# When the rows of h are requested, and which queue loads a tile's records, in a sparse graph attention layer

## The chip, the cores and the metric

One NeuronCore of a Trainium2 chip runs the whole kernel as one launch. The metric is the time of the device in microseconds (us), lower is better. The five engines are named as in the profile: PE (TensorE, matrix products and transposes), PEld (its weight loads), DVE (VectorE), ACT (ScalarE), POOL (GpSimd) and SP (SyncE, which here only issues DMAs). Each engine executes its own instructions in the order in which the built program lists them.

## The reference

```python
def layer_norm(x, scale, bias):
    mu = jnp.mean(x, axis=-1, keepdims=True)
    var = jnp.mean(jnp.square(x - mu), axis=-1, keepdims=True)
    return (x - mu) * jax.lax.rsqrt(var + EPS) * scale + bias

hs = layer_norm(x, ln1_scale, ln1_bias)          # 4096 x 512
ht = layer_norm(h_target, ln1_scale, ln1_bias)   # 4096 x 512
q = (ht @ Wq + bq).reshape(T, 8, 64) / sqrt(64)
k = (hs @ Wk + bk).reshape(S, 8, 64)
v = (hs @ Wv + bv).reshape(S, 8, 64)
logits = jnp.einsum('thd,shd->hts', q, k)
logits = jnp.where(adj[None] != 0, logits, NEG)
ctx = jnp.einsum('hts,shd->thd', softmax(logits), v).reshape(T, 512)
ht = layer_norm(ht + ctx @ Wo + bo, ln2_scale, ln2_bias)
ff = gelu(ht @ W1) @ W2                          # 512 -> 2048 -> 512
out = layernorm(x + ht + ff)
```

All numbers are float32. The adjacency is 4096 x 4096 int32 with about 17 ones in a row: each target row attends to few sources. The node mask, all ones here, is left out above.

## The kernel before

**Two stages.** In the first, up to about 300 us, the keys and values of all source rows are computed and written to a DRAM table `kvd` (one row of 1024 numbers for each source), while VectorE and ScalarE turn the rows of the adjacency into lists of neighbours. The target rows are sorted by their number of neighbours, in two halves (16 tiles of 128 rows each, A and B), and a record of each row (its degree, its index TGT, the scale and shift of its first norm, up to 24 neighbours) is scattered to DRAM in the sorted order. The lists of the second half are finished during the second stage, up to about 680 us.

**The second stage** goes through 32 tiles of 128 target rows. A tile has between 11 and 39 slots, a slot being one neighbour for each of its 128 rows. The slots are taken three at a time: a slot group (the list `SG`, 211 of them). The steps that the text speaks of, with their lines in the profile:

- *Record load* (L978, tile `rec`, seven buffers): the 128 records of a tile are loaded from DRAM. `prefetch` issues it two tiles ahead, on GpSimd's queue for the first two tiles and on SyncE's for the others. The buffer comes free when the output rows of the tile seven before have been scattered, since the scatter takes its indices from the record.
- *Request of h* (L964, a helper that issues every indirect gather; tile `tq`, three buffers): the 128 rows of `h_target` that the record names, by an indirect DMA on GpSimd's queue.
- *Norm of h* (L990, ScalarE), four transposes (L994, PE), their copies with scale and bias (L997, ScalarE), the product with Wq (L1003, PE) and the scaled q (L1008, VectorE). The generator `front` issues these steps one by one; each `yield` in it is a turn, and there are two turns for each slot group.
- *Requests of kv* (L964, tile `kv`): one indirect gather of 128 rows (512 KB) for each slot into a ring of 17 places (20 from half B on), issued by `issue(k)` four slot groups ahead of their use (five in half B).
- *Logits and values*: the product of q with the keys (L1197) and its sums (L1201) on VectorE, the exponentials on ScalarE (L1205, L1214 and L1178), the values weighted on VectorE (L1161, L1165) and, for the third slot of a group, on ScalarE (L1181, eight instructions), and the sum over the slots by accumulating transposes on PE (L1169, tile `cps`).
- *End of a tile* (`finish`): the sums' reciprocals (L1073, L1079, L1081, L1084), h added by transposes of `tq` (L1092) and the product with Wo (L1096), which are the last readers of that `tq` buffer, then the second norm and its transposes (L1122).
- *Feed-forward* (`feed`): tiles in pairs, with the products L1304 (w1) and L1313 (w2) on PE and the gelu (L1307) on ScalarE. ScalarE loads a table each time it changes between gelu and the exponentials. The rows of x are requested (L964, tile `xt`), the last norm is taken (L1260 to L1277) and the output rows are scattered by an indirect DMA on GpSimd's queue (L1281, `out_dram`).

**Order.** The attention and the feed-forward are generators; `_weave` takes the one with the smaller sum of estimated costs next, and so writes the order of the program. The framework's scheduler then places each engine's instructions by that order as a priority and by when their inputs and buffers are ready in its own estimate, so that an instruction can stand earlier in its engine's queue than the program asks. The order is fixed when the kernel is built. Where buffers are reused, the waits follow from the framework.

In the kernel before, `issue(k)` for the first slot group of a tile issues, in this order, the record load of the tile two ahead, the request of its own h (which begins its `front`), and its first kv requests:

```python
if j0 == 0:
    prefetch(i + 2)
    if i not in tqs:
        fronts[i] = front(i)
        step(fronts, i)
```

Of the kernel before, what the change touches and what calls it, by code (L numbers as in the profile page):

```python
# [17 lines left out]
P = 128  # L18
# [360 lines left out]
RW = E0 + RE  # L379
# [64 lines left out]
def adj_resnorm_kernel(  # L444
# [33 lines left out]
    nc = tc.nc  # L478
# [22 lines left out]
    NA, NBT = len(CAPS_A), len(CAPS_B)  # L501
# [11 lines left out]
    recs_d = [dram.tile([n * P, RW], I32, name=f"rec{i}") for i, (_, n) in enumerate(PARTS)]  # L513
# [19 lines left out]
    with tc.tile_pool(name="keep", bufs=1) as keep:  # L533
# [17 lines left out]
        with ExitStack() as late:  # L551
# [409 lines left out]
            recs, tqs, h2Ts, done, ready = {}, {}, {}, set(), []  # L961
# [6 lines left out]
            def prefetch(i):  # L968
                if i >= NT or i in recs:
                    return  # L970
                r0 = TILES[i][0]
                part = 1 if r0 >= PARTS[1][0] * P else 0
                assert part in done
                r0 -= PARTS[part][0] * P
                rec = sp.tile([P, E0 + MAXE], I32, name="rec", bufs=7)

                eng = nc.gpsimd if i < 2 else nc.sync
                eng.dma_start(rec[:, :RW], recs_d[part][r0:r0 + P, :])  # L978
                recs[i] = rec

            def front(i):


                rec = recs[i]
                tq = sp.tile([P, 2 * D], F32, name="tq", bufs=3)
                t = tq[:, :D]
                gather(t, h_target, rec[:, TGT:TGT + 1])
                yield
                m = rec[:, RST:RST + 2].bitcast(F32)
                nc.scalar.activation(t, t, AF.Identity, bias=m[:, 1:2], scale=m[:, 0:1])  # L990
                yield
                pt = ps.tile([P, KC, P], F32, name="t", bufs=2)
                for kc in range(KC):
                    nc.tensor.transpose(pt[:, kc, :], t[:, kc * P:(kc + 1) * P], ident)  # L994
                hT = tq[:, D:].rearrange("p (c t) -> p c t", c=KC)
                for kc in range(KC):
                    nc.scalar.activation(hT[:, kc, :], pt[:, kc, :], AF.Identity,  # L997
                                         bias=b1r[:, kc:kc + 1], scale=s1c[:, kc:kc + 1])
                yield
                yield  # L1000
                pq = ps.tile([P, D], F32, name="t", bufs=2)
                for kc in range(KC):
                    nc.tensor.matmul(pq, hT[:, kc, :], wq[:, kc, :], start=kc == 0,  # L1003
                                     stop=kc == KC - 1)
                yield
                yield
                yield
                nc.vector.scalar_tensor_tensor(tq[:, :D], pq, HD ** -0.5, bqr,  # L1008
                                               op0=ALU.mult, op1=ALU.add)
                tqs[i] = tq  # L1010


            SG = [(i, j0, min(S, cap - j0)) for i, (_, cap) in enumerate(TILES)
                  for j0 in range(0, cap, S)]
            kvs, rests, fronts = {}, {}, {}
            place = [0]
            for i, _, n in SG:
                if place[-1] + n > RING[i >= NA]:
                    place[-1] = 0
                place.append(place[-1] + n)  # L1020
            first_b = next(k for k, (i, _, _) in enumerate(SG) if i >= NA)
            issued = [0]

            def step(gens, i):

                if i in gens and next(gens[i], StopIteration) is StopIteration:
                    del gens[i]

            def request(k):
# [3 lines left out]
                while issued[0] <= min(k + ahead, len(SG) - 1):  # L1033
# [3 lines left out]
                        assert not mine & set(range(place[m], place[m] + SG[m][2]))  # L1037
                    issued[0] += 1

            def issue(k):  # L1040

                i, j0, n = SG[k]
                if j0 == 0:
                    prefetch(i + 2)
                    if i not in tqs:
                        fronts[i] = front(i)
                        step(fronts, i)
                    if TILES[i][1] > RE:
                        rests[i] = rest_of(i)
                        next(rests[i])  # L1050
                elif j0 + n > 12 and i in rests:
                    for _ in rests.pop(i):
                        pass
                kvs[k] = ring[:, place[k]:place[k] + n, :]
                for j in range(n):
                    gather(kvs[k][:, j, :], kvd[0:N + 1, :], recs[i][:, E0 + j0 + j:E0 + j0 + j + 1])

            def finish(i, p, cps, group, hs, mv):


                rec, tq, cap = recs[i], tqs.pop(i), TILES[i][1]
# [33 lines left out]
                for c in range(KC):  # L1095
                    nc.tensor.matmul(pa, ct[:, c, :], wo[:, c, :], start=False,  # L1096
                                     stop=c == KC - 1, skip_group_check=True)
                yield
                h = sp.tile([P, D], F32, name="h")
                nc.scalar.copy(h, pa)  # L1100
# [33 lines left out]
            def first_fronts():  # L1134

                for i in range(EARLY):
                    prefetch(i)
                for i in range(EARLY):
                    fronts[i] = front(i)
# [216 lines left out]
                for g in gens:  # L1356
                    yield from g

            EARLY = 2
            WAIT = 40.0  # L1360
            AHEAD = 4
            UNIT = 60.0
# [102 lines left out]
```

## Time and profile before

| | |
|---|---|
| median of 4 runs | 1855.67 us (1853.2 to 1859.01) |
| the profiled execution's own time | 1857.45 us |
| its span, first to last instruction | 1855.6 us |
| mean granted TensorE clock | 0.956 |
| busy: PE, DVE, ACT, POOL | 91%, 77%, 65%, 52% of the span |
| kv requests (L964) | 603, 746.9 us busy, 1239 ns each in the mean |
| requests of h (L964, tile tq) | 32, median 962 ns |
| record loads on SyncE (L978) | 30, 14.5 KB each, median 320 ns |
| record loads on GpSimd (L978) | 2, 585 ns each |
| norms of h (L990) | 32, median 813 ns |

How to read it: all durations come from one execution, recorded by the hardware profiler. Busy is the time in which an engine executes, without the time in which it waits. "Idle before" is the time that an engine stood before an instruction, with the instruction or DMA that released it. PE's busy time is that of a pipeline: two products that overlap count once. The granted clock is the share of TensorE's full speed that the chip allowed. A line such as L964 is that of a helper, so its instructions are told apart by their tiles.

### The profile page before, as it was taken

How to read it: one execution, taken by the hardware profiler on the slowest of the kernel's cores; microseconds unless marked ns; L12 is line 12 of the kernel's file. 1: busy time of each engine (PE TensorE's matmuls, PEld its weight loads, DVE VectorE, ACT ScalarE, POOL GpSimd, SP SyncE). 2: the span in 40 equal slices, each digit the busy share in tenths (PEclk: the TensorE clock that was granted, in tenths of full speed). 3: DMA queues.
4: the chain of work that ended last, by engine and by line, in shares of the span. 5: the costliest groups of instructions: out<-in, count | busy, mean ns of one | idle time of the engine just before them, and what ended most of it. 6: DMA issues, size and time to landing. Idle time of an engine off the chain costs nothing. (4 is left out here: it accounts for less than half of the span.)

```text
span 1855.6 us, 22978 instructions
## 1 busy us (share of the span) xinstructions
PE 1692.0 (91%) x7030; PEld 1105.2 (60%) x7030; DVE 1429.3 (77%) x2596; ACT 1211.0 (65%) x3111; POOL 956.5 (52%) x804
## 2 busy tenths in 40 slices
PE   7989874697988989999998989799999999999995
PEld 3434432465655656767666666576666666656663
DVE  6989855999989838777968999788979698778000
ACT  5767634577877637676768877676868677756211
POOL 1000143835546577647568788766667566643101
PEclk9999987789989999999999999899999999999998
DMA  9999959978876648768778788778677776763000
GB/s 351 363 374 378 346 165 345 355 265 328 303 269 204 233 121 304 256 227 276 255 265 304 270 300 301 245 260 263 221 249 243 250 261 217 249 206 114 23 0 25
DMA packets 147757, 463.28 MB, mean 250 GB/s; under 512 B 24468, under 2 KB 29160, under 8 KB 147624
## 3 DMA queue, kind: packets, MB, share of 16 engines
q0 software_dynamic: 95696, 342.19, 54.0%
q1 hardware_dynamic: 44112, 96.44, 14.7%
q10 hardware_dynamic: 7816, 23.08, 3.3%
q8 instruction: 58, 0.95, 0.2%
q14 instruction: 75, 0.61, 0.1%
HBM read 430.76 MB, written 30.89 MB: 249 GB/s over the span
## 5 line engine op out<-in xcount | busy, mean ns | idle before, releaser
L964 POOL DMA_INDIRECT kv<-kvd,rec x603 | 746.9, 1239 | 406.3 <-PE cps L1169 163.1
L1313 PE MATMUL po<-w,gt 128*128 128x512 f32 x1024 | 469.4, 601 | 8.0 <-ACT gt L1307 7.2
L1304 PE MATMUL pf<-h2T,w 128*128 128x256 f32 (+1 forms) x2176 | 470.2, 370 | 0.0
L1197 DVE TENSOR_TENSOR kv<-kv,tq 128x1536 f32<-128x1536 f32 (+2 forms) x211 | 352.1, 1676 | 110.3 <-DMA kv<-kvd,rec 96.1
L1304 PEld LDWEIGHTS pf<-h2T,w 128*128 128x128 f32 x2176 | 392.9, 193 | 66.6 <-issue 21.1
L1181 ACT ACTIVATE kv<-kv,pa 128x64 f32<-128x64 f32 x1520 | 391.4, 336 | 4.5
L1201 DVE TENSOR_REDUCE lg<-kv 128x24 f32<-128x1536 f32 (+2 forms) x211 | 350.3, 1667 | 6.8 <-ACT pa L1178 5.6
L1313 PEld LDWEIGHTS po<-w,gt 128*128 128x128 f32 x1024 | 190.1, 193 | 206.0 <-issue 197.5
L1169 PEld LDWEIGHTS cps<-ident,kv 128*128 128x128 f32 x2008 | 240.7, 146 | 108.3 <-issue 51.5
L1169 PE MATMUL cps<-ident,kv 128*128 128x128 f32 x2008 | 265.2, 281 | 42.2 <-DVE kv L1161 37.0
L1161 DVE TENSOR_TENSOR kv<-kv,p 128x1024 f32<-128x1024 f32 (+1 forms) x211 | 250.7, 1193 | 18.1 <-ACT p L1205 11.5
L687 POOL TENSOR_TENSOR n_rs<-n_ve,mhalf 128x2 f32<-128x2 f32 (+2 forms) x51 | 53.0, 1039 | 354.5 <-DVE n_ve L680 188.7
L728 ACT ACTIVATE kv<-kv 128x1024 uint8<-128x1024 int32 x128 | 134.8, 1054 | 81.3 <-DMA kv<-in_adj_dram 40.6
L929 PE MATMUL pq<-wk,h2T 128*128 128x512 f32 x256 | 125.7, 635 | 12.8 <-ACT tq L931 5.9
L1307 ACT ACTIVATE gt<-pf 128x512 f32<-128x512 f32 x128 | 76.3, 596 | 91.9 <-PE pf L1304 88.5
L735 DVE MAX8 cand<-kv 128x8 uint16<-128x103 uint16 (+1 forms) x640 | 129.8, 251 | 0.5
L1307 ACT ACT_TABLE_LOAD x99 | 127.0, 1283 | 1.6
L1003 PE MATMUL t<-wq,tq 128*128 128x512 f32 x256 | 118.8, 606 | 9.1 <-ACT tq L997 8.5
L1205 ACT ACTIVATE p<-lg 128x24 f32<-128x24 f32 (+2 forms) x179 | 39.0, 218 | 133.8 <-DVE lg L1201 87.9
L929 PE MATMUL pq<-wv,h2T 128*128 128x512 f32 x256 | 115.2, 593 | 1.5 <-ACT tq L931 1.5
L1096 PE MATMUL t<-wo,rb 128*128 128x512 f32 x256 | 115.5, 592 | 0.0
L990 ACT ACTIVATE tq<-tq,rec 128x512 f32<-128x512 f32 x32 | 26.0, 812 | 110.2 <-DMA tq<-in_L_gnn_h_target_dram,rec 109.8
(156 smaller groups left out, 1572.9 us busy)
## 6 DMA issues: line engine op xcount, KB each, us to landing
kv<-in_adj_dram SPq DMA_DIRECT2D x128, 512.0 KB
kvd<-tq ACTq DMA_DIRECT2D x24, 512.0 KB
kv<-kvd,rec POOLq DMA_INDIRECT x603
kv<-in_L_gnn_h_target_dram SPq DMA_DIRECT2D x32, 256.0 KB
kv<-in_x_dram SPq DMA_DIRECT2D x15, 512.0 KB
rest_d<-gid SPq DMA_DIRECT2D x32, 160.0 KB
w<-in_L_gnn_W_dram SPq DMA_DIRECT2D x4, 1024.0 KB
kvd<-kv ACTq DMA_DIRECT2D x8, 512.0 KB
```

What stands on the lines that cost most here:

```text
L728: nc.scalar.activation(sg, a, AF.Sign, accum_out=dpart[:, i, h:h + 1])
L735: nc.vector.max(cand[:, h * SQ + s, :], wd[:, w0:w1])
L929: nc.tensor.matmul(pkv, hT[:, kc, j * P:(j + 1) * P], w[:, kc, :], start=kc == 0, stop=kc == KC - 1)
L964: nc.gpsimd.indirect_dma_start(out=dst, out_offset=None, in_=table[:, :], in_offset=bass.IndirectOffsetOnAxis(ap=idx, axis=0))
L1161: nc.vector.tensor_tensor(v4, v4, p[:, j0:j0 + m, :].unsqueeze(3) .to_broadcast([P, m, H, HD]), ALU.mult)
L1169: nc.tensor.matmul(cps[:, c, :], kv[:, j, D + c * P:D + (c + 1) * P], ident, is_transpose=True, start=j0 + j == 0 and c == 0, stop=j0 + n ...
L1181: nc.scalar.mul(v, v, pa[:, hd:hd + 1])
L1197: nc.vector.tensor_tensor(kv[:, :n, :D], kv[:, :n, :D], tq[:, :D].unsqueeze(1).to_broadcast([P, n, D]), ALU.mult)
L1201: nc.vector.tensor_reduce(lg[:, :n, :], kv[:, :n, :D].rearrange("p j (h d) -> p j h d", h=H), AX.X, ALU.add)
L1304: nc.tensor.matmul(pf[:, k, :], w1[(f0 + k) // KC][:, kc, (f0 + k) % KC * P:((f0 + k) % KC + 1) * P], h2T[:, kc, :w], start=kc == 0, stop= ...
L1307: nc.scalar.activation(gt, pf, AF.Gelu_apprx_tanh)
L1313: nc.tensor.matmul(po[j], gt[:, k, j * P:(j + 1) * P], w2[(f0 + k) // KC][:, (f0 + k) % KC, :], start=False, stop=f0 + k == FC - 1, skip_g ...
```

## The change

The request of h for a tile is issued up to two slot groups sooner: before the kv requests of slot group k, `issue(k)` looks at the groups k+1 and k+2, and where one is the first of a tile, it begins that tile's `front`, provided that the tile three before has had its last product with `tq` issued (`turned`). To make up for it, `front` yields two more turns for each slot group of the lead before the norm, and in half B after its first tile two more in any case. All record loads go to GpSimd's queue. The rest is as before.

```diff
-                eng = nc.gpsimd if i < 2 else nc.sync
-                eng.dma_start(rec[:, :RW], recs_d[part][r0:r0 + P, :])
+                nc.gpsimd.dma_start(rec[:, :RW], recs_d[part][r0:r0 + P, :])
                 recs[i] = rec
 
-            def front(i):
+            def front(i, idle=0):
...
                 gather(t, h_target, rec[:, TGT:TGT + 1])
-                yield
+                for _ in range(1 + idle):
+                    yield
                 m = rec[:, RST:RST + 2].bitcast(F32)
                 nc.scalar.activation(t, t, AF.Identity, bias=m[:, 1:2], scale=m[:, 0:1])
...
+            EARLY = 2
...
+            begun_fronts, turned = set(range(EARLY)), set()
...
+            def begin(i, lead):
+
+                if i not in begun_fronts:
+                    begun_fronts.add(i)
+                    fronts[i] = front(i, 2 * lead + (2 if i > NA else 0))
+                    step(fronts, i)
+
             def issue(k):
 
+                for d in (1, 2):
+                    if k + d < len(SG) and SG[k + d][1] == 0 and SG[k + d][0] - 3 in turned:
+                        begin(SG[k + d][0], d)
                 i, j0, n = SG[k]
                 if j0 == 0:
                     prefetch(i + 2)
-                    if i not in tqs:
-                        fronts[i] = front(i)
-                        step(fronts, i)
+                    begin(i, 0)
...
                     nc.tensor.matmul(pa, ct[:, c, :], wo[:, c, :], start=False,
                                      stop=c == KC - 1, skip_group_check=True)
+                turned.add(i)
                 yield
```

`EARLY = 2` only moves up from further down in the function.

## The prediction

> **What bounds the kernel now.** I read the page first, for the share of each engine and the clock, then the waits, and then, for each place where TensorE stood still, the timeline of all engines around it.
>
> ```profile
> span 1855.6 us, 22978 instructions
> ...
> PE 1692.0 (91%) x7030; PEld 1105.2 (60%) x7030; DVE 1429.3 (77%) x2596; ACT 1211.0 (65%) x3111; POOL 956.5 (52%) x804
> ...
> PE   7989874697988989999998989799999999999995
> ...
> PEclk9999987789989999999999999899999999999998
> ```
>
> TensorE is the bound: from 700 us to 1700 us it is busy in nearly every slice. What can still be won is the few places where it stands, and the half clock that follows such a place (granted clock 0.91 from 1100 to 1200, against 1.00 from 1200 to 1600). The waits say which stream is late:
>
> ```profile
> POOL kv L964 <- PE cps L1169: 163.1, 87, 15.6
> ...
> ACT tq L990 <- DMA tq<-in_L_gnn_h_target_dram,rec: 109.8, 25, 11.7
> ...
> DVE kv L1197 <- DMA kv<-kvd,rec: 96.1, 32, 12.3
> ...
> POOL xt L964 <- DMA out_dram<-xt,rec: 21.8, 13, 4.5
> ...
> PE t L994 <- ACT tq L990: 20.4, 3, 9.6
> ```
>
> The columns are total us, times, longest. The second line is the target of the change: ScalarE stands 109.8 us at the norm of a row block of h (L990) that has not landed. The last line is what TensorE itself loses to it: 20.4 us at three tiles (8, 18 and 20). The largest, tile 20, in the timelines of PE, ACT and POOL:
>
> ```profile
> 1180.11 1.04 PE L1169 MATMUL cps<-ident,kv 128*128 128x128 f32 x8
> 1190.75 1.11 PE L994 MATMUL t<-ident,tq 128*128 128x128 f32 x4 [9.60 <-ACT tq L990]
> ...
> 1189.88 0.81 ACT L990 ACTIVATE tq<-tq,rec 128x512 f32<-128x512 f32 x1 [9.04 <-DMA tq<-in_L_gnn_h_target_dram,rec]
> ...
> 1179.23 3.98 POOL L964 DMA_INDIRECT kv<-kvd,rec  x1 [0.31 <-issue]
> ...
> 1184.77 1.30 POOL L1281 DMA_INDIRECT out_dram<-xt,rec  x1 [0.30 <-issue]
> 1186.38 0.96 POOL L964 DMA_INDIRECT tq<-in_L_gnn_h_target_dram,rec  x1 [0.30 <-issue]
> ```
>
> GpSimd asked for the h rows at 1186.38, with no idle time before it: the request is late because GpSimd's queue is full. In its timeline no gap is over 0.8 us from 1043 to 1196. So an earlier place in that queue helps, and anything put ahead of it hurts.
>
> **The change, part by part.** The order in which the two built kernels issue their instructions, compared queue by queue without a run, tells what moves.
>
> *The h request.* It is asked for sooner in the program, but its tile has three buffers, and it waits for TensorE to be done with the tile three before. Counted in kv requests ahead of it on GpSimd, 29 of the 32 stand within two of where they stood. Tile 18 moves from behind 352 to behind 333 (19 x (1.239 mean + 0.30 gap) = 29 us), tile 19 four sooner, tile 17 six later. On ScalarE the norm keeps its place to a little over one slot group for all but tiles 18, 19 and 30. Tiles 3 and 4 come two requests sooner (3.1 us): VectorE bounds that stretch, so I take nothing, and keep -3.
>
> *The record loads.* Thirty leave SyncE, where they wait 906.2 us for out_dram at L978 with little behind them: once, from 492 to 497 us, an adjacency load stood 4.9 us behind one. That is worth 0 to -4.9; I take 0, since TensorE has no gap over 1.1 us from 445 to 527. The price on GpSimd is in the two that stand there now:
>
> ```profile
> L978 POOL DMA_DIRECT2D rec<-rec x2 | 1.2, 585 | 1.8 <-DMA rec<-R,kv 1.8
> ```
>
> That is 0.585 + 0.30 gap = 0.89 us each, 27 us in all. Neither of the two ran beside VectorE's two-operand products, in which a kv request grows from a median 0.948 to as much as 4.20 us; by that ratio of mean to median (1239/948) a load is 0.76 + 0.30 = 1.06. I take 0.89 and keep 1.06 to 4.5 (4.20 + 0.30) for the range; below nothing it can't be, as each is an instruction more on that queue. They stand in pairs around the x requests, straight ahead of the first h request of a pair of tiles: request, record, x, record, x, h. The wait for an output scatter to land, which the x request bears now (2.24 us at tile 8), passes to the record in front of it and is not new there.
>
> The Trainium skill speaks against this half: "DMA: Bandwidth & Descriptors", section "SWDGE vs HWDGE vs iDMA", gives plain loads to SP or ACT and keeps GpSimd for the irregular ones, and "SBUF — State Buffer", section "SBUF: two separate sides", has a GpSimd DMA's descriptors starve while VectorE holds the shared port. The long kv requests agree; by the rule the change would only lose at every pair.
>
> *The first steps of a tile from 17 on.* On TensorE the transposes (L994) and q products (L1003) of tiles 17 to 31 go one piece of work later, mostly 8 kv transposes (8 x 0.109 = 0.9, by the distance of their starts in the timeline) and 8 passes of L1313 (8 x 0.429 = 3.4) or 16 of L1304 (16 x 0.216 = 3.5): 4.3 us. VectorE's reading of q (L1008) keeps its place among the slot groups.
>
> Now the sum, against the profiled execution's 1857.45 (span 1855.6).
> 1. Tiles 18 and 20. Tile 18's stall (4.96 us) goes with its request 29 us sooner. Tile 20's request comes later by four record loads (3.5) and one x request that now stands before it (1.25): 4.8, so its transposes start at 1195.6. But TensorE by then has done 0.9 + 3.5 + 3.4 + 0.4 + 3.4 = 11.6 us of work (L1169, L1304, L1313, L1092, L1096) that now comes after them. Gain 11.6 - 4.8 = 6.8; tile 18's gain lies inside it, since GpSimd's full queue sets that time. Two gaps become one, and of the 9 us that a clock of 0.91 takes from 100 us I count 3.4 back: -10.2. Bounds: 0 (the stall only moves) and -23 (both gaps and the clock go).
> 2. L1003 stood 2.38, 2.32 and 2.06 us for ScalarE's copy L997 at tiles 26, 27 and 30; one piece later it finds it done: -6.8 (0 if ScalarE slips as far).
> 3. Tile 8 waits already 5.89 us; two record loads more: +1.8.
> 4. Tile 16: the same two loads put the kv rows for 958 us later, and the first slot of tile 15 reached TensorE only 0.6 us ahead: +1.2. At tiles 10, 12 and 14 TensorE reached the transposes 12 to 26 us after the norm, which covers 1.8: nothing.
> 5. Tiles 17 and 19: q is 4.3 us later and VectorE had 1.4 and 2.5 us in hand, so it stands 2.9 and 1.8 where it is 92% busy (147.21 of 160 us): +3.0 of the 4.7, as the reserve ahead of TensorE was 2 to 7 us. From tile 20 on that reserve is 7 us and more: nothing.
> 6. ScalarE gets ten more table loads by the order, at 1.28 us: 12.8 us, all after 760 us. It is 73% busy there, and from tile 20 on 9 us and more ahead of TensorE: nothing. Six fall before 920 us, where the first slot of a tile is only 2 to 3 us ahead: 0 to 7.7, kept for the range.
> Sum: -10.2 - 6.8 + 1.8 + 1.2 + 3.0 = -11.0, so 1846.5 beside the profiled time and 1844.7 beside the median of 1855.67. I say 1846.
>
> **Rivals.**
> *Slower.* The wait for output scatters. From the start of the out_dram request to the release of the next took 5.6 us at tile 8 and 5.5 at 946 us. Where GpSimd now fills that with h and kv requests (tile 20), the records close the gap: 5.5 less one request (1.3) plus 1.8 is 6 us at each of 15 pairs, 90 us of GpSimd. It decides where the kv rows lead VectorE by less than 6 us beyond the 3.4 that a request needs, as from 815 to 960. If a third reaches TensorE, 30 - 17 = +13: 1870. For it: that queue is full for 150 us. Against: 163.1 us in which kv requests wait for TensorE, a cover for most pairs. 0.33.
> *No change.* VectorE at 92% from 1040 to 1200 takes over: gain 1 fails, the rest is -0.8: 1857. 0.17.
> *It does what it says.* If the real clock let the h rows come two slot groups sooner everywhere, L994's 20.4, L1003's 6.8 and half of the half clock go: some -45, 1812. Against it stands the order, in which the requests do not move. 0.07.
> *My sum*, 1833 to 1850: 0.43.
>
> **How the numbers follow.** 0.3% is 5.6 us, about what a measurement of this kernel can tell from no change. Faster is my case and the large one, 0.50; same 0.17; slower 0.33. From my case's gains at their bounds (-23 - 6.8) the low end is 1828; the high end, 1872, takes in the slower rival.
>
> **What would show it.** Right: the PE wait on L990 at tile 18 gone, one gap of about 11 us at tile 20, no gap over 2 us at L1003 after 1400, ScalarE's wait at L990 still near 100 us, 30 record loads under 1.1 us. Wrong: that wait far below 60 us (the requests did come sooner); the record loads waiting 3 us and more each, with VectorE's wait for kv rows well above 96.1 us (the slower rival); VectorE's wait at L1008 well above 38.4 us (part 5 too small).

## The result and the profile after

The changed kernel takes 1855.15 us (median of 52 runs, 1839.59 to 1868.24) against 1858.43 us for the kernel before (median of 78). The ratio is 0.9979, with a 95% interval of 0.997 to 0.9988: 3.9 us less of 1858 by the ratio. The sign is that of the forecast; the forecast gain was 9.7 us beside the median, more than twice as much. The profiled execution of the changed kernel took 1857.43 us, as long as the 1857.45 us of the one before, so the two profiles show where time moved, not how much was won.

The page of the changed kernel, the same rows as were shown of before:

```profile
span 1855.7 us, 22879 instructions
...
PE 1694.8 (91%) x7030; PEld 1105.3 (60%) x7030; DVE 1429.4 (77%) x2596; ACT 1221.6 (66%) x3121; POOL 972.7 (52%) x834
...
PE   7989874697988989999998989989999999999997
...
PEclk9999987698999989999999999999999999999999
```

GpSimd has 30 instructions and 16.2 us more. Of TensorE's waits before, the largest (9.60 us, tile 20) is down to 2.21; one near 990 is longer (5.83 us for 3.18), and others are new: 4.58 us near 902, 3.77 near 1093 and 3.62 near 1309. The waits of the changed kernel:

```profile
POOL kv L964 <- PE cps L1181: 163.9, 79, 16.3
ACT tq L990 <- DMA tq<-in_L_gnn_h_target_dram,rec: 136.2, 27, 12.9
...
DVE kv L1209 <- DMA kv<-kvd,rec: 73.0, 28, 10.9
...
DVE tq L1008 <- PE t L1003: 45.5, 9, 10.0
...
POOL rec L977 <- DMA out_dram<-xt,rec: 28.0, 12, 4.6
...
PE t L1003 <- ACT tq L997: 14.3, 6, 4.6
...
PE t L994 <- ACT tq L990: 9.4, 3, 5.8
```

ScalarE's wait for the h rows grew from 109.8 to 136.2 us: the rows did not come sooner. TensorE's wait at the transposes (L994) fell from 20.4 to 9.4 us, its wait at the q product (L1003) rose from 8.5 to 14.3. The group of the record loads:

```profile
L977 POOL DMA_DIRECT2D rec<-rec x32 | 18.6, 581 | 29.8 <-DMA out_dram<-xt,rec 28.0 <-DMA rec<-R,kv 1.8
```

Each load took 581 ns, as the two of before did (585). The wait for the output scatters stands in front of them now (28.0 us, and 3.5 in front of the x requests, against 21.8 there before). Apart from such waits GpSimd does not stand before a plain load. Its gap of 0.30 us comes before indirect requests only:

```profile
587.67 1.61 POOL L964 DMA_INDIRECT xt<-in_x_dram,rec  x1 [0.31 <-issue]
589.28 0.59 POOL L977 DMA_DIRECT2D rec<-rec  x1
590.16 1.94 POOL L964 DMA_INDIRECT xt<-in_x_dram,rec  x1 [0.30 <-issue]
```

So a load lengthens GpSimd's queue by 0.58 us, and thirty of them by 17 us.

The end of the program differs too. The last lines of PE's timeline, before and after:

```profile
core 0 of [0], span 1855.6 us
...
1828.29 7.03 PE L1313 MATMUL po<-w,gt 128*128 128x512 f32 x16
```

```profile
core 0 of [0], span 1855.7 us
...
1835.82 7.03 PE L1325 MATMUL po<-w,gt 128*128 128x512 f32 x16
```

Before, TensorE ended at 1835.3 and the program 20.3 us later; after, at 1842.8 and 12.9 us later. In this execution TensorE lost 7.5 us and the end gave as much back. The prediction had no term for that end.

### The profile page after: what moved, and what is told of

Same layout as the page of the kernel before. It is cut to its first block, busy times and chain, and to the rows that moved or that the text cites. A ratio compares the mean times of both kernels' runs of the same rounds, so it can differ in the third digit from the quotient of the medians.

```text
span 1855.7 us, 22879 instructions
## 1 busy us (share of the span) xinstructions
PE 1694.8 (91%) x7030; PEld 1105.3 (60%) x7030; DVE 1429.4 (77%) x2596; ACT 1221.6 (66%) x3121; POOL 972.7 (52%) x834
## 5 line engine op out<-in xcount | busy, mean ns | idle before, releaser
L1181 PE MATMUL cps<-ident,kv 128*128 128x128 f32 x2008 | 269.7, 283 | 54.0 <-DVE kv L1173 45.0
L687 POOL TENSOR_TENSOR n_rs<-n_ve,mhalf 128x2 f32<-128x2 f32 (+2 forms) x51 | 48.3, 948 | 345.0 <-DVE n_ve L680 174.3
L1003 PE MATMUL t<-wq,tq 128*128 128x512 f32 x256 | 122.9, 624 | 14.7 <-ACT tq L997 14.3
L990 ACT ACTIVATE tq<-tq,rec 128x512 f32<-128x512 f32 x32 | 26.0, 813 | 143.2 <-DMA tq<-in_L_gnn_h_target_dram,rec 136.2
```

What stands on the lines that cost most here:

```text
L1181: nc.tensor.matmul(cps[:, c, :], kv[:, j, D + c * P:D + (c + 1) * P], ident, is_transpose=True, start=j0 + j == 0 and c == 0, stop=j0 + n ...
```

## The experiments

Differences in us are the ratio less one, times 1858. "End" is the span less the end of TensorE's last product, in the run's own profile. A time "at TensorE" is the difference in time with the difference of the ends taken out.

| kernel | median us | ratio (95%) | us | end |
|---|---|---|---|---|
| the change | 1855.15 | 0.9979 (0.997 to 0.9988) | -3.9 | 12.9 |
| e1 records alone | 1870.66 | 1.0072 (1.0049 to 1.0094) | +13.4 | 12.5 |
| e2 early begin and idle, no records | 1844.44 | 0.9927 (0.9905 to 0.9949) | -13.6 | 20.4 |
| e3 without the two further turns | 1875.88 | 1.0085 (1.0055 to 1.0115) | +15.8 | 12.5 |
| e4 the two further turns alone | 1846.91 | 0.994 (0.9914 to 0.9966) | -11.1 | 20.2 |
| e5 records in ScalarE's queue | 1841.38 | 0.991 (0.9878 to 0.9942) | -16.7 | 20.3 |
| e6 e2 and 30 loads in stage 1 | 1845.65 | 0.9922 (0.9896 to 0.9948) | -14.5 | 12.7 |
| e7 e1 with each load twice | 1881.51 | 1.0107 (1.007 to 1.0143) | +19.9 | 12.9 |
| e8 record loads a slot group later | 1854.53 | 0.9979 (0.9953 to 1.0004) | -3.9 | 12.7 |
| e9 e2 and 30 idle loads | 1854.58 | 0.9984 (0.9968 to 1.0001) | -3.0 | 21.1 |
| e10 e5 and 30 idle loads | 1855.45 | 0.9982 (0.996 to 1.0003) | -3.3 | 20.9 |
| e11 records of odd tiles | 1849.73 | 0.9949 (0.9928 to 0.997) | -9.5 | 11.5 |
| e12 e1 and 30 loads in stage 1 | 1868.40 | 1.0061 (1.0034 to 1.0087) | +11.3 | 15.8 |
| e13 records of tiles 14 to 21 alone | 1865.55 | 1.0041 (1.0019 to 1.0062) | +7.6 | 21.2 |
| e14 records of the other tiles alone | 1856.42 | 0.9993 (0.9974 to 1.0013) | -1.3 | 12.3 |
| e15 e4 for tiles 17 to 20 only | 1851.22 | 0.9962 (0.9944 to 0.9981) | -7.1 | 20.2 |
| e16 e4 for tiles 21 to 31 only | 1848.93 | 0.995 (0.9926 to 0.9973) | -9.3 | 20.3 |
| e17 e5 and 20 late writes | 1826.03 | 0.984 (0.9805 to 0.9874) | -29.7 | 11.5 |
| e18 before and 20 late writes | 1848.48 | 0.9948 (0.9927 to 0.9969) | -9.7 | 11.7 |

### The two halves of the change (e1 to e4)

**e1, the records alone** (against the kernel before):

```diff
-                eng = nc.gpsimd if i < 2 else nc.sync
-                eng.dma_start(rec[:, :RW], recs_d[part][r0:r0 + P, :])
+                nc.gpsimd.dma_start(rec[:, :RW], recs_d[part][r0:r0 + P, :])
```

> Only the thirty record loads move to GpSimd's queue; begin, idle and order of all else as before. In the changed kernel TensorE's last product ended 7.5 us later than before (1842.8 against 1835.3 us), and the end of the program behind it took 7.4 us less (12.9 against 20.3). Theory A: the records' share of that is about 5 us, paid where GpSimd's queue is full (tile 8 and around 985 us), and the end of the program varies from execution to execution whatever the kernel: slower than before by 3 to 6 us. Rival B: the records cost nothing on TensorE's path: within 1.5 us of before. Rival C: the short end comes from the records no longer being in SyncE's queue: faster by 2 us or more, with an end of about 13 us in the profile.

Slower by 13.4 us, with an end of 12.5 us: all three theories fall in part. The records cost far more than theory A had, and theory C is right that the end follows the record loads. At TensorE's last product the price is 13.4 + 7.8 = 21 us. One way by which a load of 0.58 us can reach TensorE is seen at tile 14. The timeline of DVE, ACT and PE in e1 (its lines stand one above those of before: L996 and L1002 for L997 and L1003):

```profile
899.08 1.23 DVE L1196 TENSOR_TENSOR kv<-kv,tq 128x1024 f32<-128x1024 f32 x1 [2.63 <-DMA kv<-kvd,rec]
900.22 1.74 DVE L1200 TENSOR_REDUCE lg<-kv 128x24 f32<-128x1536 f32 x1
...
902.00 0.22 ACT L1204 ACTIVATE p<-lg 128x24 f32<-128x24 f32 x1 [4.72 <-DVE lg L1200]
...
902.35 2.02 ACT L1180 ACTIVATE kv<-kv,pa 128x64 f32<-128x64 f32 x8
...
904.85 1.51 ACT L996 ACTIVATE tq<-t,b1r,cols 128x128 f32<-128x128 f32 x4
905.36 1.12 PE L1002 MATMUL t<-wq,tq 128*128 128x512 f32 x2 [3.96 <-ACT tq L996]
```

GpSimd has no more than its 0.30 us gaps here, so the kv rows come late by what was put ahead of them. VectorE waits 2.63 us for them, the exponential (L1204) waits for VectorE's sums, and the copy that TensorE's q product needs stands behind that exponential in ScalarE's queue: TensorE waits 3.96 us. In the kernel before the same product waited 1.10:

```profile
896.08 3.70 PE L1003 MATMUL t<-wq,tq 128*128 128x512 f32 x8 [1.10 <-ACT tq L997]
```

This is the way by which a late kv row arrives, and no proof that the loads alone make it late: the same product waited 3.3 us in e2 and 5.4 in e16, where the thirty record loads are not on GpSimd. The place is tight, and one profile doesn't say what tips it.

The largest single wait of TensorE in e1 that the kernel before does not have goes another way. GpSimd also computes the reciprocal root of the norms (L687, tile `n_rs`), and this instruction stands in the same queue as the requests:

```profile
1116.06 0.73 POOL L687 TENSOR_TENSOR n_rs<-n_ve,mhalf 128x2 f32<-128x2 f32 x1
1116.83 0.16 DVE L692 SCALAR_TENSOR_TENSOR n_nm<-mv,n_rs 128x2 f32<-128x2 f32 x1 [4.08 <-POOL n_rs L687]
1117.02 1.52 ACT L1112 ACTIVATE h<-h,n_nm,n_rs 128x512 f32<-128x512 f32 x2 [3.90 <-DVE n_nm L692]
1117.89 0.48 PE L1121 MATMUL t<-ident,h 128*128 128x128 f32 x1 [5.59 <-ACT h L1112]
```

Its input was there at 1107.7, and the request then running and five more went ahead of it. VectorE, ScalarE and TensorE each waited for it. In the kernel before VectorE waited 0.62 us at this place and TensorE not at all. It, too, is one profile.

Where the price falls is seen at the first q product of each tile. In e1 it begins 6.0 us later than before at tile 8, 9.3 at tile 14, 13.4 at 17, 22.4 at 20, 25.0 at 24 and 24.3 at 31. In e18 below, which up to 1690 us is the kernel before in all but one instruction's place, the same comparison wanders by up to 4.3 us. So the price is paid by tile 24, most clearly from 17 to 20. Of the 24 us by which TensorE's last product is later in this profile, 16.6 are more time in which TensorE stands (99.8 us after 330 us, against 83.2); in the same stretch it runs 119 us at a granted clock of 0.5, against 95.

Moving the loads changes more than one queue. By the traces some 80 of ScalarE's instructions and some 25 of VectorE's stand elsewhere in their queues than before, while TensorE's order is the same. That this reordering has a part in the price is not excluded by e1; e9 below speaks for most of it being GpSimd's time. The size of the price rests on the times.

**e2, the early begin and idle alone:** the changed kernel with the two lines of the record load as in the kernel before.

> Only the early begin with its idle steps; the record loads stay in SyncE's queue as before. Theory A (records cost 5 us, the rest of the change gains): faster than before by 6 to 9 us, 1850 beside 1858. Rival B (records cost nothing): the same as the changed kernel, 3 to 4 us faster than before. Rival C (the short end of the program comes from the records in GpSimd's queue): slower than before by 3 us or more, with an end of about 20 us in the profile. By all of them TensorE's waits at the q product (L1003) at tiles 14, 20, 22 and 24 are there as in the changed kernel, and those at tiles 26, 27 and 30 are gone.

Faster by 13.6 us, more than theory A had; end 20.4 us. The two halves add up within their intervals: -13.6 + 13.4 is -0.2 where the change has -3.9. On top of the early begin the records cost 0.9979 / 0.9927, or 0.52% and 9.7 us, and with the shorter end 9.7 + 7.5 = 17 us at TensorE. The waits at L1003 were as expected at tiles 14 and 22 (3.3 and 2.5 us), but not at tiles 20 and 24 (0 and 0.4).

**e3, the change without the further turns:**

```diff
-                    fronts[i] = front(i, 2 * lead + (2 if i > NA else 0))
+                    fronts[i] = front(i, 2 * lead)
```

> The change without the two further idle steps for tiles from 17 on: records in GpSimd's queue, early begin with idle by the lead alone. By the order, the norm of tile 23 and of tile 25 is then behind the copy L997 of tile 22 and 24 again, and the h request of tile 18 stands behind 347 kv requests, not 333. Theory A: TensorE's waits at L1003 for tiles 20, 22 and 24 (2.6, 3.6 and 2.4 us) go, those at 26, 27 and 30 (about 2 us each) come back, tile 18's and tile 20's waits at L994 come back (5 and 9 us or more): slower than the changed kernel by 6 to 10 us. Rival: the two further steps bring nothing on balance: within 2 us of the changed kernel.

15.8 us slower than before, 19.7 slower than the change, much more than theory A's 6 to 10; TensorE waits at L994 again, 4.4 us at tile 19 and 11.0 at tile 20. It is close to the records alone (e1, +13.4): with the records on GpSimd, the early begin without the further turns brings nothing that these runs can tell.

**e4, the further turns alone** (against the kernel before):

```diff
-                        fronts[i] = front(i)
+                        fronts[i] = front(i, 2 if i > NA else 0)
```

with `front` yielding `1 + idle` times as in the change.

> The kernel before with one thing added: the norm of tiles from 17 on comes two steps later (the further idle steps without the early begin, records in SyncE's queue). By the order this alone moves the h request of tile 18 from behind 352 to behind 332 kv requests and puts TensorE's work on q one piece later. Theory A: the early begin does next to nothing by itself, and this is the whole of the reordering: within 2 us of the kernel with the early begin and records on SyncE. Rival: the early begin matters (an h request that stands ready earlier in its queue): 4 us or more slower than that kernel.

11.1 us faster, 2.5 us from e2: a little over theory A's bound of 2, well inside the intervals, and short of the rival's 4. What the change is named for, an earlier request of h, brings nothing that these runs can tell; what gains is the norm two turns later in the second half.

### Per load, or where the queue is full? (e7 to e14)

**e7, each record load followed by a second into a DRAM place that nobody reads:**

```diff
...
                 nc.gpsimd.dma_start(rec[:, :RW], recs_d[part][r0:r0 + P, :])
+                if i >= 2:
+                    nc.gpsimd.dma_start(twin_d[part][r0:r0 + P, :], recs_d[part][r0:r0 + P, :])
```

> Only the records on GpSimd, and each of the thirty loads followed by a second one of the same rows into a scratch place in DRAM, which nobody waits for. The first thirty cost 20 us at TensorE's last product by the medians (12.3 more in time with an end that is 7.6 shorter) for 27 us of GpSimd's queue. If the price is GpSimd's time, the second thirty cost about as much again: 1888, and 1880 to 1895. If the price is the wait for the output scatter that the first load takes over, the second thirty cost little: 1872 to 1876.

+19.9 us, 6.5 more than e1: by the ratio, 1878 us, between the two expectations (the median of 1881.5 is at the low edge of the first). The profile shows one wait in it that e1 does not have, 10.81 us at the transposes of tile 10, whose h request the added loads moved from behind 145 to behind 155 kv requests. The interval of the difference is wider than the 6.5, so this run does not show a price per load.

**e8, the record loads at the second slot group of a tile:**

```diff
-                if j0 == 0:
+                if j0 == S:
                     prefetch(i + 2)
+                if j0 == 0:
                     begin(i, 0)
```

> The changed kernel with the record of tile i + 2 loaded at the second slot group of tile i instead of the first, so that no record stands between the x request and the h request. If the price of the records is their place directly ahead of the h request and behind the output scatter, most of it goes: 1845 or less. If it is GpSimd's time anywhere in a full queue, 1853 to 1857, as the changed kernel.

No different from the change (0.9979 both), and it could not be: the edit did not reach the queues. In the trace of e8 the instructions of GpSimd, VectorE, TensorE and SyncE stand in the same order as in the change, with the records ahead of the h requests as there, and ScalarE's order differs by one instruction. The framework's scheduler put the loads where they had been. So e8 is a second measurement of the change, and says nothing about the place.

**e9, e2 and thirty loads that nobody waits for:**

```diff
...
                     gather(kvs[k][:, j, :], kvd[0:N + 1, :], recs[i][:, E0 + j0 + j:E0 + j0 + j + 1])
+                if k == len(SG) - 1:
+                    for j in range(30):
+                        r = (j % PARTS[1][1]) * P
+                        nc.gpsimd.dma_start(twin_d[j * P:(j + 1) * P, :], recs_d[1][r:r + P, :])
```

> Early begin and idle with the records on SyncE (1844.4), and thirty plain loads on GpSimd after its last kv request, into a scratch place in DRAM that nobody reads; GpSimd is nearly idle from there. If the end of the program hangs on the number of GpSimd's requests (32 plain loads: 12.5 to 12.9 us in five kernels; 2: 20.2 to 20.4 in four), it is about 12.7 us, and since the loads stand behind all requests that TensorE waits for, the time is 1837. If the 9 us that TensorE lost when the same number stood in stage 1 come from their number and not from their place, the time stays near 1845.

The loads did not go where the expectation had them. They wait for nothing but the records, so the framework's scheduler placed them as soon as these were there, from 678.5 to 743.8 us, between kv requests:

```profile
L1073 POOL DMA_DIRECT2D twin<-rec x30 | 15.2, 512 | 2.7 <-DMA rec<-R,kv 2.4
```

What the run shows instead: loads that nobody needs cost 0.57% against e2, 10.7 us, with an end that is no shorter (21.1). No consumer waits for them, GpSimd's wait for the scatters is no longer (28.7 us, against 35.3 in e2), and few instructions change places (3 on ScalarE, 1 on VectorE), so their price is most likely the 15.2 us of GpSimd's time; their traffic was not tried apart from it. **e10** is the same on e5 and agrees (+0.73% against it, 13.5 us).

> The same thirty late loads on the kernel with the records in ScalarE's queue (1841.4 with an end of 20.4 us): 1834 if the end is shortened and TensorE loses nothing, 1841 or more if it does. The better of the two would be the fastest version of this study.

**e11, the records of odd tiles on GpSimd, the others on SyncE, the rest as the change:**

> The changed kernel with the records of odd tiles alone on GpSimd (15 instead of 30 moved) and the others on SyncE. By TensorE's last product (median time less the end of the program) the records on GpSimd cost about 19 us with early begin, so half of them cost 9 to 10 if the price is GpSimd's time: TensorE's part at half way, and the time 1846 with a short end, 1854 with a long one. If the first few cost most (a phase, not a price per load), 1851 and more with a short end. The end itself tells whether 15 more loads are enough to shorten it.

0.9949 with an end of 11.5 us, so against e2 4.1 + 8.9 = 13 us at TensorE for 15 loads, where thirty cost 17. By these middle values that is not in proportion to their number, but intervals of 4 us on each ratio don't exclude it.

**e6 and e12, thirty small loads in stage 1,** where GpSimd has little to do, on e2 and on e1:

```diff
...
+                spare = wp.tile([P, 30, 8], F32, name="spare")
+                for j in range(30):
+                    nc.gpsimd.dma_start(spare[:, j, :], x[j * P:(j + 1) * P, :8])
                 nc.gpsimd.memset(lower, -1.0)
```

> Early begin and idle, records on SyncE, and thirty small plain loads (128 rows of 32 bytes of x, never read) in GpSimd's queue during the lists of stage 1, where that queue is nearly empty. If the short end of the program hangs on how many plain loads GpSimd's queue has had, the end is about 12.7 us and the time 1837; if it hangs on SyncE's queue, or on when they are sent, the end stays 20.3 us and the time 1844 to 1846.

> The records on GpSimd without early begin (1870.7), and the thirty small loads of stage 1 besides. If each early load costs TensorE 0.3 us, as the comparison on the kernel with the records on SyncE would have it (9 us), the time is 1880. If that loss was tied to the shortening of the end, which has taken place here already, or was chance, the time stays at 1869 to 1872.

In e6 the end is 12.7 us, by which the loads' number counts for it, not their place or SyncE's queue; but the time did not follow (-14.5 for -13.6). The end gave 7.7 us and the time gained 0.9, so TensorE ended 6.8 us later than in e2. In e12 the time fell by 2.1 us though the end is 3.3 longer, so TensorE ended 5.4 us earlier than in e1. One loss and one gain, each about as large as its interval: loads in an idle queue have no price that these runs can tell, and why e6 did not become faster stays open.

**e13 and e14, the records of tiles 14 to 21 alone on GpSimd, and all but those** (against the kernel before):

```diff
-                eng = nc.gpsimd if i < 2 else nc.sync
+                eng = nc.gpsimd if i < 2 or 14 <= i < 22 else nc.sync
```

> The kernel before with the records of tiles 14 to 21 alone on GpSimd (8 of the 30; they are loaded between about 857 and 1194 us). Moving all thirty cost 12.3 us in time and, with an end of the program that is 7.8 us shorter, 20 us at TensorE's last product; in that profile TensorE fell behind at tile 14 (4.6 us near 900), near 990 (3) and from 1075 to 1130 (8). Theory of places: these eight loads cost most of it, 12 to 16 us at TensorE, and the end stays about 20.5 us (743 requests): 1870 to 1874. Rival, a price per load wherever it stands: 8/30 of 20 us, 5 us: 1863.

> The complement: the records of all tiles but 14 to 21 on GpSimd (22 of the 30). Theory of places: 4 to 7 us at TensorE, with an end of about 12 us (757 requests): 1854 to 1857. Rival, a price per load: 22/30 of 20, 15 us at TensorE: 1865.

e13: +7.6 with an end 0.9 longer, 6.7 us at TensorE for 8 loads. e14: -1.3 with an end 8.0 shorter, 6.7 us for 22. Neither theory had its number: the price is unevenly spread (0.84 against 0.30 us a load), but not as far as the theory of places said, and the two make 13 of the 21 us of all thirty.

### The two gains, apart (e15, e16)

```diff
+                        fronts[i] = front(i, 2 if NA < i < 21 else 0)
```

is e15, and `2 if i > 20 else 0` is e16, each in the place of the line of e4.

> The kernel before with the two further idle steps for tiles 17 to 20 alone, records on SyncE: steps 1 and 5 of the prediction's sum without the records. If step 1 holds (two gaps at L994 become one or none, and the half clock with them): 13.7 less 3.0, 10.7 us faster, 1848. Rival: the gain of the further steps comes from the later tiles: within 3 us of before.

> The complement: the two further steps for tiles 21 to 31 alone, step 2 of the sum. If step 2 holds (TensorE's waits at L1003 for tiles 26, 27 and 30 go and none comes): 6.8 us faster, 1851. Rival: the waits that come at tiles 22 and 24, where the next tile's norm then stands ahead of the copy on ScalarE, take it back: within 2 us of before.

e15: -7.1 of the 10.7 expected. The waits at L994 of tiles 18 and 20 are gone, and others have taken their place. The timelines of ACT and PE in e15 (L991, L1004, L1082, L1166 and L1170 are L990, L1003, L1081, L1165 and L1169 of before):

```profile
1069.17 0.81 ACT L991 ACTIVATE tq<-tq,rec 128x512 f32<-128x512 f32 x1 [6.86 <-DMA tq<-in_L_gnn_h_target_dram,rec]
...
1071.79 0.58 ACT L1082 COPY rb<-t 128x512 f32<-128x512 f32 x1
...
1073.74 1.09 PE L1170 MATMUL cps<-ident,kv 128*128 128x128 f32 x8 [2.32 <-DVE kv L1166]
1078.81 1.97 PE L1170 MATMUL cps<-ident,kv 128*128 128x128 f32 x8 [3.97 <-DVE kv L1166]
...
1195.65 4.64 PE L1004 MATMUL t<-wq,tq 128*128 128x512 f32 x5 [4.31 <-ACT tq L998]
```

ScalarE now meets tile 18's norm while it still has work of the tile before behind it. It stands 6.86 us for the h rows; the copy L1082 comes after that, VectorE stands 6.04 us for the copy, and TensorE twice for VectorE. At tile 20 TensorE waits for the copy L998 in place of the transposes. e16: -9.3 where 6.8 was expected, within its interval. The waits at tiles 26, 27 and 30 are gone, and those feared at 22 and 24 did not appear, though the order is the one feared and the norm of tile 23 waits 3.99 us there.

### Another queue, and the end of the program (e5, e17, e18)

**e5, the change with the records in ScalarE's queue:**

```diff
-                nc.gpsimd.dma_start(rec[:, :RW], recs_d[part][r0:r0 + P, :])
+                eng = nc.gpsimd if i < 2 else nc.scalar
+                eng.dma_start(rec[:, :RW], recs_d[part][r0:r0 + P, :])
```

> The changed kernel with the thirty record loads in ScalarE's queue: off SyncE, but not on GpSimd. Two questions. The end of the program behind TensorE's last product took 12.5 to 12.9 us in the three kernels with the records on GpSimd and 20.2 to 20.4 us in the three with them on SyncE. If the records' absence from SyncE's queue makes it short, it is about 12.7 us here; if their presence in GpSimd's makes it short, about 20.3. And GpSimd's queue is free of them, so TensorE's last product should end near 1828 us, as with the records on SyncE. Times: 1837 by the first (1844.4 less 7.6), 1844 by the second; a wait of the record load in ScalarE's queue for the scatter would show as 1850 and more.

-16.7 us with an end of 20.3: the long end returns although SyncE has no record loads, so it is GpSimd's loads that shorten it. The time is no worse than with the records on SyncE (-13.6); a part of the difference may be order, since here ScalarE's, VectorE's and TensorE's orders differ from those of e2 as well.

**e17, e5 and twenty writes that can't be sent before the last h2T, and e18, the same on the kernel before:**

```diff
...
                 group, h2T = GROUPS[g], h2Ts.pop(g)
+                if g == len(GROUPS) - 1:
+                    for j in range(20):
+                        nc.gpsimd.dma_start(late_d[j * P:(j + 1) * P, :], h2T[:, 0, :8])
```

> Early begin and idle, records in ScalarE's queue (1841.4), and twenty small writes (128 rows of 32 bytes of the last h2T, into a place that nobody reads) on GpSimd behind the last h2T, from about 1690 us on, where GpSimd has 6 us of work in 100. With 735 requests on GpSimd the end of the program behind TensorE's last product took 20.2 to 20.4 us, with 750 and 757 of them 11.5 and 12.3. If the number of requests sets the end, it is about 12 here and, as nothing stands behind the writes that TensorE waits for, the time is 8 us shorter: 1833. If the end is set by something else that the loads changed, it stays 20.3 and the time 1841 to 1843. In this version ScalarE takes the loads, GpSimd's full queue is spared, and the end is short: the fastest of the study if it holds.

> The kernel before with those twenty late writes and nothing else: the effect on the end alone. 8 us faster than before, with an end of about 12 us for 20.3, if the number of GpSimd's requests sets it; within 1 us of before, with an end of 20.3 us, if not.

e18 gains 9.7 us, e17 29.7 and 13 more than e5, with ends of 11.7 and 11.5 us, 8.6 and 8.8 shorter. The orders are those of before and of e5 but for the writes (and one instruction of ScalarE in e18), so the writes shorten the end; the other 4 us of e17 lie within its interval. What counts is GpSimd's number of requests, though not of every kind: e9 and e10 have 765, as the change has, and keep the long end, since loads from DRAM to DRAM count for less (last section). e17's groups and its last product:

```profile
L1309 POOL DMA_DIRECT2D late_d<-h2T x20 | 10.7, 544 | 12.8 <-ACT h2T L1140 12.3 <-issue 0.5
```

```profile
core 0 of [0], span 1826.8 us
...
1808.31 7.03 PE L1330 MATMUL po<-w,gt 128*128 128x512 f32 x16
```

The writes wait 12.3 us for h2T and stand behind everything that TensorE needs. e17 is the fastest kernel of the study, 1826.03 us (median of 5), 1.6% below the kernel before. The writes have no use but this; e5 is what remains without them.

## Why the prediction was wrong

The forecast's sign was right, by luck, and its size was not. By halves, its sum was -17.5 us for the reordering (13.7 for tiles 18 and 20 without the record loads, 6.8 for L1003, less 3.0) and +6.5 for the records (3.5 at tile 20, 1.8, 1.2). Measured: -13.6 for the reordering, +17 at TensorE for the records on top of it, -7.5 at the end of the program: -3.9. Without the end, of which the sum knew nothing, the change would have been 3.6 us slower.

**The failed step is the price of the records.** The sum let 6.5 us of it reach TensorE, and 17 to 21 us reached it (17 on the early begin, 21 in e1). "That is 0.585 + 0.30 gap = 0.89 us each, 27 us in all" has the load right (0.581) and the gap wrong: a plain load has none, and thirty of them lengthen GpSimd's queue by 17 us. So what arrived is not a part of the 27 us, as the sum had it, but as much as the loads take, or more. The sentence that failed is "At tiles 10, 12 and 14 TensorE reached the transposes 12 to 26 us after the norm, which covers 1.8: nothing." The cover was sought for the h row alone. In e1 two other ways lead from a late queue to TensorE: the kv rows behind the loads, by way of VectorE's sums, ScalarE's exponential and the copy queued behind it, and the second norm's `n_rs` on GpSimd itself. e1 is 13.4 us late at tile 17, where the sum had 3.0 (steps 3 and 4), and loses 9.0 more up to tile 20, where it had 3.5. That each of the two ways makes its share, and which tile pays what, stays open: it rests on single profiles.

**The end of the program** was a term that the sum left out. The prediction let no gain in for the record loads: "below nothing it can't be, as each is an instruction more on that queue". But at the end of the program, thirty of them were worth 7.5 us (e18 shows it alone: 9.7 us by twenty writes).

**Step 1 (tiles 18 and 20).** "Tile 18's stall (4.96 us) goes with its request 29 us sooner" is the sentence that failed. TensorE's wait at the transposes went, but ScalarE's wait in front of them did not; it stands 9.43 us at the norm, sooner in the program than before, and what is queued behind it is then late. ACT and PE of the changed kernel:

```profile
1091.21 0.82 ACT L990 ACTIVATE tq<-tq,rec 128x512 f32<-128x512 f32 x1 [9.43 <-DMA tq<-in_L_gnn_h_target_dram,rec]
1091.93 2.00 ACT L1193 ACTIVATE kv<-kv,pa 128x64 f32<-128x64 f32 x8
...
1092.56 1.90 PE L1181 MATMUL cps<-ident,kv 128*128 128x128 f32 x4 [3.77 <-ACT kv L1193]
```

Of tile 18's 4.96 us, 3.77 are lost here. At tile 20 there is no single gap of about 11 us but 2.21 at L994 and 2.57 at L1003. The step followed the waiting product and not the waiting engine in front of it: it did not ask what else stands behind the norm on ScalarE. With step 5 it was 10.7 us and came to 7.1.

**Step 2 (L1003)** held: 9.3 us alone, where 6.8 was said; no gap over 2 us at L1003 after 1400 us in the changed kernel. But that was forecast for tiles 26, 27 and 30 only. In the changed kernel tiles 14, 20, 22 and 24 wait 4.58, 2.57, 3.62 and 2.38 us at the same product. At tile 22 the order shows why, and the reading of it missed that: the next tile's norm now stands ahead of the copy in ScalarE's queue, and waits for its own h rows. ACT's timeline of the changed kernel:

```profile
1306.68 0.81 ACT L990 ACTIVATE tq<-tq,rec 128x512 f32<-128x512 f32 x1 [4.06 <-DMA tq<-in_L_gnn_h_target_dram,rec]
...
1308.62 1.48 ACT L997 ACTIVATE tq<-t,b1r,cols 128x128 f32<-128x128 f32 x4
```

In the kernel before, L997 stands ahead of that norm at tiles 22 and 24. In e16 the same order costs TensorE 0.35 us at tile 22, in e2 2.5, both without the thirty loads on GpSimd. So the order alone does not decide it; what does stays open.

**Steps 3 to 6.** Tile 8 waits 5.8 us, as before, and was reached 1.1 us later where 1.8 was said. Step 5 named the wrong tiles: VectorE does not stand for q at 17 and 19, but 7.7 and 10.0 us at 22 and 24, behind the waits just shown (8.0 and 8.2 in e2). The ten table loads came, at 1.28 us each, in e2 and e4 as well, which gained all the same; their price was not tried by itself.

**The rivals.** The slower one had the right half and the wrong mechanism: the records do cost more than 13 us, but not through the wait for the scatters. GpSimd stood 21.8 us for them before and 23.1 in e1, 35.3 in e2 and 31.5 in the change, so the records add next to none, and e9's loads, which wait for no scatter, cost as much. "It does what it says" is ruled out: ScalarE's wait for h rose. The rule weighed in the prediction from the Trainium skill, "DMA: Bandwidth & Descriptors", section "SWDGE vs HWDGE vs iDMA", leaves plain loads to SP and ACT. The runs agree: the early begin has 0.9927 with the records on SyncE, 0.991 on ScalarE and 0.9979 on GpSimd. The reason given in "SBUF — State Buffer", section "SBUF: two separate sides", is not what the runs show for these loads: none was held up in the changed kernel. Eight of the thirty ran wholly beside a VectorE TENSOR_TENSOR and took 0.58 to 0.59 us, and the longest of all took 0.61. The upper price of 4.5 us a load, kept for the range, did not come.

**What stays open.** Why 8 loads and 22 loads make 13 us and all thirty 21, and why e6 gave nothing for its shorter end. With intervals of 2 to 7 us to either side of each difference, these may be small or nothing. A run that moves the loads and leaves every other instruction's place as it was would tell the loads' time from the reordering; there is none among these, and e9, with added loads, comes nearest. Whether the further turns would gain more with four buffers of `tq` wasn't tried.

## What to carry to other kernels

An instruction that is added to a full queue is paid by everything behind it there, not by its own consumer: follow what stands behind it, arithmetic as well as requests, through each engine's queue to the bound engine before calling it covered. Read the built order of the queues after an edit: e8 changed the source and not the queue. Undo each half of a change by itself, since here a gain of 13.6 us and a loss of 13.4 hid each other in one result of 3.9. And look at the end of a program as at any other stage: 20 us passed there behind the last product, and eight of them could be had without touching the computation.

## What the hardware showed that was not expected

The end of the program hangs on how many DMAs GpSimd has sent. Behind its last request GpSimd has two instructions that the views don't list but the trace holds, INC_SWDGE_SEM and a DRAIN. Together they took 10.33 us in the kernel before and 2.61 in the changed kernel, 7.7 us apart where the ends are 7.5 apart. The DRAIN took 8.16 us in all six kernels with 735 requests, 8.81 with 743, 0.73 with 750, 1.14 in both with 755, 1.30 with 757, 1.95 in all five with 765 (e9 and e10 aside), and 4.40 in e12 with 795. That is as if it took 0.081 us for each request since a count that starts again between 743 and 750: (8.81 - 8.16) / 8, (1.95 - 0.73) / 15 and (4.40 - 1.95) / 30 agree. Loads from DRAM to DRAM count less: thirty of them added 0.57 us in e9 (8.73 in e9 and e10, beside the 8.16 of 735) and 0.41 in e7, as much as seven and five of the others.

The same count seems to show within the run. In the kernel before, GpSimd stands 1.14, 2.87 and 2.89 us for nothing that the profile names after its requests 113, 325 and 537, which are 212 apart, and 749 would be next:

```profile
488.82 0.94 POOL L964 DMA_INDIRECT kv<-kvd,rec  x1 [1.14 <-issue]
...
915.78 1.49 POOL L964 DMA_INDIRECT kv<-kvd,rec  x1 [2.87 <-issue]
...
1299.85 0.94 POOL L964 DMA_INDIRECT kv<-kvd,rec  x1 [2.89 <-issue]
```

In e5 it stood 7.63 us after request 537. Other kernels stop after other requests, most of them again 113 and a multiple of 106: the change 1.92 us after request 643, e11 1.13, 2.73 and 2.85 us after 325, 643 and 749. In e9 the stops come after 348 and 560, 23 later than 325 and 537, which is right if the thirty loads ahead of them count as seven, as the DRAIN has it. That both are one store of requests that is turned over, and starts again at 749, fits all these numbers but is argued from them, not shown.
